# Where the softplus's sums and the fourth state's input run, in the last scan of a four-layer kernel

## The chip, the core and the metric

The kernel runs on one core of one Trainium2 chip, as one program without arithmetic on the host. The metric is the device time of one execution in microseconds; the median of three runs is given, and lower is better.

## The reference

Four residual layers work on four images of 128 channels and 128 x 128 pixels, in fp32. Each is x + layer(groupnorm(x)):

- layer 0: a deformable convolution (offsets from a 3 x 3 convolution, bilinear sampling at nine taps, a product with the weights);
- layer 1: a dilated 5 x 7 convolution to 16 channels and back to 128;
- layer 2: half of the channels go through a depthwise convolution, half through a selective scan in four directions over all 16384 pixels;
- layer 3: a 3 x 3 convolution less a difference of neighbours.

The change lies in layer 2's scan. Cut to it:

```python
dts = jnp.einsum('bkrl,kdr->bkdl', dts, dt_w)
delta = jax.nn.softplus(dts + dt_b[None, :, :, None])
def step(h, inp):
    u, d, b, c = inp
    dA = jnp.exp(d[..., None] * A)
    h = h * dA + (d * u)[..., None] * b[:, :, None, :]
    y = jnp.einsum('bkcn,bkn->bkc', h, c)
    return (h, y)
_, ys = lax.scan(step, h0, (u_l, d_l, B_l, C_l))
```

There are 128 channels, four directions k and 16 states n; the step runs over 16384 positions.

## The kernel before

**Blocks.** The scan of one image and direction is cut into 32 blocks of 512 positions, so there are 4 x 4 x 32 = 512 blocks in all, numbered through. A block has 128 channels x 16 states = 2048 rows. They are laid on the 128 partitions as four groups (g = 0 to 3) of 32 channels, each channel on four partitions; a group has four tiles along the free axis (ng = 0 to 3), called states here. One group is thus a tile h of 128 x 4 x 512.

**One group.** inputs_up (L893, ACT) copies delta*u of the group from the SBUF tile spread to the PSUM tile dub. DVE multiplies dub with the B values (L996), which makes the scan's inputs for the four states at once. ACT makes the decays exp(delta*A) into the PSUM tiles pa (L919), one a state, a little ahead. DVE scans each state (L1044). ACT saves the last column (carry, L953), POOL multiplies h by the C values, two states at a time (outputs, L959), and PE sums them over the partitions into yacc (sums, L933). One of the four inputs can be made apart: last_input (L899) has POOL multiply state 3 straight from spread, half a group ahead, and L996 then covers three states (1536 elements) in place of four (2048).

**The block after next.** While block t is scanned, the generator prepare(t + 2) makes its delta, one step at each state: PE makes pdt, ACT makes |x|, relu, exp(-|x|), 1 + e, ln(1 + e) (L841 to L854) and subtracts 1 again (L856). The softplus is relu + ln(1 + e) + (e - ((1 + e) - 1)), the last bracket a correction. These sums are made either by POOL in three instructions (L872, L874, L876), or on PE as four products with the identity or its negative into a PSUM tile psum (L867), copied back by ACT (L869). POOL then multiplies delta by u (L878); the result goes to DRAM and comes back spread out over the partitions. pdt, pxbc, psum and dub are all of one tag ("dub") of a pool with one buffer, so each waits for the reader of the one before.

**What runs beside.** The scan is the main loop. Between its states it pulls steps from the layers of the neighbouring images: beside the scan of image b run layer2_post and layer3 of image b - 1, and layer0, layer1 and layer2_pre of image b + 1. The wrapper loads() writes into beside["busy"] which engine the running stage loads: "POOL" for layer0 (whose gathers POOL issues), "PE" for layer1, layer2_pre and, in the earlier scans, layer2_post and layer3. In the last scan there is no next image; there layer2_post and layer3 of image 2 and layer2_post of image 3 run under the label None. So does the table that image 1's layer0 gathers from, early in the first scan.

**Order.** The instructions of each engine run in the order in which the program emits them (keep_order at the end holds it). Within a group of block t the loop over the states emits, for state 1: decays, outputs of the group before (second half), inputs_up for the next group if g > 1, sums of two groups before, a step of prepare; for state 2: carry_on, decays, last_input for the next group, a step of prepare, inputs_up if g < 2; for state 3: a step of prepare, outputs of this group (first half), sums of the group before. At states 1, 2 and 3 the scan itself is emitted after these. With on_pe the four PE products of prepare fall on state 1 of group 2 and the copy L869 on state 2 of that group, and inputs_up comes at state 2 in every group. Before the change on_pe holds beside layer0 alone, and last_input runs for odd g, wherever DVE doesn't take over part of the outputs (on_vector, again beside layer0 alone).

Of the kernel before, what the change touches and what calls it, by code (L numbers as in the profile page):

```python
# [111 lines left out]
def conv_preact_kernel(ctx: ExitStack, tc: tile.TileContext, a: dict, nb: int):  # L112
# [9 lines left out]
    def load(pool, src, shape, name, **kw):  # L122
        t = pool.tile(shape, F32, name=name, **kw)
        nc.sync.dma_start(t, src)
        return t
# [5 lines left out]
    beside = {}  # L131
# [64 lines left out]
    def blk(t, i):  # L196
        return t[:, i * N : (i + 1) * N]
# [593 lines left out]
    def scan(pull):  # L791
# [4 lines left out]
        seq = []  # L796
# [9 lines left out]
        def decays(at):  # L806

            beside["decays"] = lambda: decays(at + 1)
            while ahead["made"] < min(at + 2, len(seq) * NST):
                decay(ahead["made"])  # L810
                ahead["made"] += 1

        def fetch(t):
            if t < len(seq):
                st, k, i, _ = seq[t]
                while st.get("out", 0) < (i + 1 if k == 0 else NBLK + 1):
                    pull()
                    tick()
                if "y" not in st:
                    st["y"] = image("yrow"), image("ycol")  # L820
                us = st["u"]
                if not stored(us[0]):
                    flush()
                blocks[t]["u"] = load(sp, blk(us[k % 2], i), [P, N], "u", bufs=2)
# [57 lines left out]
        def spread_steps(t, g):  # L882

            blocks[t]["p", g] = p = sp.tile([P, 2, N], F32, name="spread", bufs=3)
            src = blocks[t]["steps"][g * Q : (g + 1) * Q]
            nc.sync.dma_start(
                p.rearrange("p j t -> p (j t)"), src.unsqueeze(1).to_broadcast([Q, P // Q, 2 * N])
            )

        def inputs_up(t, g):  # L890

            blocks[t]["pdu", g] = p = pss.tile([P, N], F32, name="dub", tag="dub")
            nc.scalar.copy(p, blocks[t]["p", g][:, 1, :])  # L893

        def last_input(t, g):

            c = blocks[t]
            c["h", g] = h = hp.tile([P, NG, N], F32, name="h")
            nc.gpsimd.tensor_mul(h[:, NG - 1, :], c["p", g][:, 1, :], c["bb"][:, NG - 1, :])  # L899

        def spread_states(t, what):

            blocks[t][what] = p = bp.tile([P, NG, N], F32, name=what)
            src = blocks[t]["bc"][("bb", "cb").index(what)].rearrange("(s n) t -> s (n t)", n=NG)
            nc.sync.dma_start(
                p.rearrange("p n t -> p (n t)"), src.unsqueeze(0).to_broadcast([Q, P // Q, NG * N])
            )
# [14 lines left out]
        def sums(t, g, half):  # L922

            c = blocks[t]
            second = seq[t][3]
            if g == 0 and half == 0:
                c["y"] = pss.tile([P, N], F32, name="yacc")
            last = g == NG - 1 and half == 1
            parts = (2 * half, 2 * half + 1)
            if half and c.get(("added", g)):  # L930
                parts = parts[:1]
            for ng in parts:
                nc.tensor.matmul(  # L933
                    c["y"], gather[:, g, :], c["h", g][:, ng, :],
                    start=g == 0 and ng == 0, stop=last and ng == parts[-1] and not second,
                )
            if last and second:
                nc.tensor.matmul(c["y"], ident, c["before"], start=False, stop=True)

        def finish(t):  # L940
            st, k, i, back = seq[t]
            y = sp.tile([P, N], F32, name="y", bufs=1)
            nc.scalar.copy(y, blocks[t]["y"])
            store(blk(st["y"][k % 2], i), y, of=st["y"])
            blocks[t] = None
            st["summed"] = t % (NDIR * NBLK) + 1 - 3 * NBLK

        def carry_on(t, g, half):

            end = 0 if seq[t][3] else N - 1  # L950
            n = g * NG + 2 * half
            h = blocks[t]["h", g][:, 2 * half : 2 * half + 2, :]
            nc.scalar.copy(blocks[t]["carry"][:, n : n + 2].unsqueeze(2), h[:, :, end : end + 1])  # L953

        def outputs(t, g, half, engine=nc.gpsimd):

            c = blocks[t]
            h = c["h", g][:, 2 * half : 2 * half + 2, :]
            engine.tensor_mul(h, h, c["cb"][:, 2 * half : 2 * half + 2, :])  # L959
            if half and g % 2 and beside.get("busy") == "PE":  # L960
                engine.tensor_add(h[:, 0, :], h[:, 0, :], h[:, 1, :])
                c["added", g] = True
# [17 lines left out]
        for t, (st, k, i, back) in enumerate(seq):  # L980
            c = blocks[t]
            carry = c["carry"]
            on_pe = beside.get("busy") == "POOL"
            more = prepare(t + 2, on_pe) if t + 2 < len(seq) else iter(())
            if t > 0:
                fetch(t + 3)
            for g in range(NG):
                then = (t, g + 1) if g + 1 < NG else (t + 1, 0)
                soon = (t, g + 2) if g + 2 < NG else (t + 1, g + 2 - NG)
                before = (t, g - 1) if g else (t - 1, NG - 1)  # L990
                earlier = (t, g - 2) if g > 1 else (t - 1, g + NG - 2)
                ready = ("h", g) in c
                if not ready:
                    c["h", g] = hp.tile([P, NG, N], F32, name="h")
                h, n = c["h", g], NG - 1 if ready else NG
                nc.vector.tensor_tensor(  # L996
                    h[:, 0:n, :], c["pdu", g].unsqueeze(1).to_broadcast([P, n, N]), c["bb"][:, 0:n, :], ALU.mult
                )
                on_vector = beside.get("busy") == "POOL"
                if before[0] >= 0:  # L1000
                    carry_on(*before, 1)
                if soon[0] < len(seq):
                    spread_steps(*soon)
                at = t * NST + g * NG
                decays(at)
                if g == 1:
                    if t + 1 < len(seq):
                        spread_states(t + 1, "bb")
                if g == 2 and t + 1 < len(seq):
                    spread_states(t + 1, "cb")  # L1010
                if g == 3 and back:
                    c["before"] = load(sp, blk(st["y"][k % 2], i), [P, N], "before", bufs=1)
                for ng in range(NG):
                    n = g * NG + ng
                    if ng == 1:
                        decays(at + 1)
                        if before[0] >= 0 and not on_vector:
                            outputs(*before, 1)
                        if g > 1 and then[0] < len(seq) and not on_pe:
                            inputs_up(*then)  # L1020
                        if earlier[0] >= 0:
                            sums(*earlier, 1)
                    if ng == 2 and g == 1 and t > 0:
                        finish(t - 1)
                    if n % NST and ng != 2:
                        next(more, None)
                    if ng == 2 and before[0] >= 0 and on_vector:
                        outputs(*before, 1, nc.vector)
                    if ng == 2:
                        carry_on(t, g, 0)  # L1030
                        decays(at + 2)
                        if g % 2 and not on_vector and then[0] < len(seq):
                            last_input(*then)
                        next(more, None)
                        if (g < 2 or on_pe) and then[0] < len(seq):
                            inputs_up(*then)
                    if ng == 3:
                        outputs(t, g, 0, nc.vector if on_vector and g == NG - 1 else nc.gpsimd)
                        if before[0] >= 0:
                            sums(*before, 0)  # L1040
                    o, f = h[:, ng, :], c["a", n]
                    if back:
                        o, f = o[:, ::-1], f[:, ::-1]
                    nc.vector.tensor_tensor_scan(o, f, o, carry[:, n : n + 1], ALU.mult, ALU.add)  # L1044
                    if ng == 3:
                        decays(at + 3)
                    yield (t * NST + n + 1) / slots
            for _ in more:
                pass
# [409 lines left out]
```

## Time and profile before

| what | value |
|---|---|
| median of three runs | 21988.68 us (21982.39 to 22019.09) |
| the profiled execution | 22048.69 us, its span 22046.9 us |
| busy over the span | PE 80%, DVE 81%, POOL 80%, ACT 74% |
| the scan on DVE, L1044 | 8192 instructions of 1267 ns |
| outputs on POOL, L959 | 3651 instructions of 2365 ns (445 more on DVE) |
| last_input on POOL, L899 | 845 instructions of 1278 ns |
| sums of the softplus on POOL, L872, L874, L876 | 423 of each, 1272 to 1283 ns |
| the same on PE, L867 | 89 blocks; each of the four products is two records of 592 ns |

An fp32 matmul stands in the trace as two records. The mean of PE's records includes the time in which one overlaps the next, so their sum is above PE's busy time. The last scan starts near 18000 us and ends near 21710 us; the convolution of image 3 follows until the end.

How to read the rows: a group's row gives line, engine and operation, what it writes and reads, the count; then busy time in us, the mean of one in ns, and how long the engine stood idle just before it and for whom. A row of the windows view gives, for a stretch of time, each engine's busy time and count of instructions, then the granted TensorE clock as a share of full speed, the busy share of the DMA engines, and GB/s.

### The profile page before, as it was taken

The page shows a single profiled execution, that of the slowest core. Times are in us where ns is not written, and L with a number is a line of the kernel's source. Part 1 is how long each engine was busy: PE and PEld are TensorE (multiplying, and loading weights), DVE is VectorE, ACT ScalarE, POOL GpSimd, SP SyncE. Part 2 cuts the span into 40 slices and gives each one's busy share as a digit, 9 for nine tenths or more (in the row PEclk, how much of TensorE's full clock was granted, in tenths as well). Part 3 has the DMA queues.
Part 4 walks back from the last instruction along what each step waited for, and adds up shares of the span by engine and source line. Part 5 has one row for each costly group of instructions (what it writes and reads, how often), then busy time and mean ns, then how long its engine had stood idle before and what let it go on. Part 6 is the DMA issues. An engine that isn't in the chain of part 4 may idle for free. (4 is left out here: it accounts for less than half of the span.)

```text
span 22046.9 us, 206313 instructions
## 1 busy us (share of the span) xinstructions
PE 17530.0 (80%) x51536; PEld 8506.2 (39%) x51536; DVE 17759.7 (81%) x18759; ACT 16420.1 (74%) x37439; POOL 17657.2 (80%) x11985
## 2 busy tenths in 40 slices
PE   4667777888878888788888887887887878778788
PEld 3444333445323333454533333344543333233333
DVE  2332688888998899888798889978889888999984
ACT  4775777888778776788868876688877877666673
POOL 3663787667899999777789999977779999999994
PEclk7888998999989999999999999999999999999999
DMA  7666678777766878777776697777776677556674
GB/s 226 189 187 185 191 241 274 245 242 246 255 207 221 237 242 266 243 246 243 246 249 216 219 262 240 257 245 240 250 252 219 221 224 228 200 202 209 214 233 134
DMA packets 2578940, 5040.76 MB, mean 229 GB/s; under 512 B 1060736, under 2 KB 1333576, under 8 KB 2435408
## 3 DMA queue, kind: packets, MB, share of 16 engines
q1 hardware_dynamic: 2209104, 3819.31, 53.2%
q0 software_dynamic: 368640, 1208.25, 18.1%
q8 instruction: 415, 6.80, 0.1%
q14 instruction: 781, 6.40, 0.1%
HBM read 4082.03 MB, written 874.52 MB: 225 GB/s over the span
## 5 line engine op out<-in xcount | busy, mean ns | idle before, releaser
L1044 DVE TENSOR_TENSOR_SCAN h<-pa,carry,h 128x512 f32<-128x512 f32 x8192 | 10011.3, 1267 | 605.7 <-ACT pa L919 386.4
L933 PE MATMUL yacc<-h,gather_sb 128*128 128x512 f32 x15264 | 7958.5, 648 | 1906.5 <-POOL h L959 1303.9
L959 POOL TENSOR_TENSOR h<-h,cb 128x1024 f32<-128x1024 f32 x3651 | 8589.1, 2365 | 622.3 <-ACT carry L953 575.2
L426 POOL DMA_INDIRECT g<-table,idx x4608 | 4535.8, 984 | 2470.2 <-issue 1174.3
L919 ACT ACTIVATE pa<-spread,neg_a 128x512 f32<-128x512 f32 x8192 | 5488.6, 682 | 109.9 <-DVE h L1044 82.3
L933 PEld LDWEIGHTS yacc<-h,gather_sb 128*128 128x128 f32 x15264 | 2967.8, 206 | 6073.5 <-issue 2925.7
L996 DVE TENSOR_TENSOR h<-dub,bb 128x2048 f32<-128x2048 f32 (+1 forms) x2048 | 4210.4, 2056 | 519.8 <-ACT dub L893 517.4
L464 PE MATMUL pst<-ident,g 128*128 128x128 f32 x9216 | 2134.8, 319 | 1327.6 <-ACT smp L469 1097.8
L440 ACT ACTIVATE g<-g,wt 128x128 f32<-128x128 f32 x9216 | 2839.4, 390 | 42.1 <-DMA g<-table,idx 38.9
L953 ACT COPY carry<-h 128x2 f32<-128x2 f32 x4096 | 769.5, 188 | 2705.7 <-DVE h L1044 2699.4
L464 PEld LDWEIGHTS pst<-ident,g 128*128 128x128 f32 x9216 | 1686.8, 224 | 2174.2 <-ACT smp L469 1614.3
L465 PE MATMUL pst<-ident,v 128*128 128x128 f32 x9216 | 2129.5, 318 | 321.9 <-DVE v L454 170.8
L451 DVE TENSOR_TENSOR pw<-pw,g 128x512 f32<-128x512 f32 x1152 | 797.0, 692 | 1961.2 <-ACT pw L440 1555.4
L465 PEld LDWEIGHTS pst<-ident,v 128*128 128x128 f32 x9216 | 1674.8, 227 | 419.2 <-DVE v L454 225.0
L440 ACT ACTIVATE pw<-g,wt 128x128 f32<-128x128 f32 x4608 | 1691.8, 367 | 131.7 <-DVE v L454 11.4
L893 ACT COPY dub<-spread 128x512 f32<-128x512 f32 x2048 | 1195.7, 584 | 302.4 <-DVE h L996 111.8
L454 DVE SCALAR_TENSOR_TENSOR v<-g,wt,pw 128x128 f32<-128x128 f32 x4608 | 1293.6, 343 | 114.4 <-issue 2.3
L475 PE MATMUL acc<-smp,w_sb 128*128 128x512 f32 x2304 | 1287.6, 642 | 21.4 <-DVE x L482 14.8
L469 ACT COPY smp<-pst 128x512 f32<-128x512 f32 x1152 | 668.1, 580 | 776.3 <-remote 578.2
L1264 PE MATMUL p<-xn,w_l_sb 128*128 128x508 f32 (+2 forms) x2304 | 1129.7, 608 | 1.8 <-ACT xn L1243 1.8
L899 POOL TENSOR_TENSOR h<-spread,bb 128x512 f32<-128x512 f32 x845 | 1079.5, 1278 | 15.9 <-DMA spread<-stepsd 10.2
L872 POOL TENSOR_TENSOR e<-e,one_e 128x512 f32<-128x512 f32 x423 | 538.2, 1272 | 486.8 <-ACT one_e L856 463.7
(183 smaller groups left out, 18935.7 us busy)
## 6 DMA issues: line engine op xcount, KB each, us to landing
spread<-stepsd SPq DMA_DIRECT2D x2048, 512.0 KB
bb<-bcd SPq DMA_DIRECT2D x512, 1024.0 KB
cb<-bcd SPq DMA_DIRECT2D x512, 1024.0 KB
stepsd<-steps SPq DMA_DIRECT2D x512, 512.0 KB
table<-gt SPq DMA_DIRECT2D x512, 256.0 KB
g<-table,idx POOLq DMA_INDIRECT x4608
u<-urow SPq DMA_DIRECT2D x256, 256.0 KB
yrow<-y SPq DMA_DIRECT2D x256, 256.0 KB
```

The source lines that it names most:

```text
L426: nc.gpsimd.indirect_dma_start(out=g[:, r].rearrange("p q c -> p (q c)"), out_offset=None, in_=table, in_offset=bass.IndirectOffsetOnAxis( ...
L440: nc.scalar.activation(pw[:, r * P : (r + 1) * P] if c == 0 else g[:, r, c, :], g[:, r, c, :], AF.Copy, scale=wv[:, r, q, k, c : c + 1],)
L454: nc.vector.scalar_tensor_tensor(v[:, r, :], g[:, r, 3, :], wv[:, r, q, k, 3:4], pw[:, r, :], ALU.mult, ALU.add)
L464: nc.tensor.matmul(dst, g[:, r, 2, :], ident, start=True, stop=False)
L465: nc.tensor.matmul(dst, v[:, r, :], ident, start=False, stop=True)
L475: nc.tensor.matmul(got["a", i], w0[:, k, :], got.pop(("c", n)), start=k == 0, stop=k == KK - 1)
L893: nc.scalar.copy(p, blocks[t]["p", g][:, 1, :])
L919: nc.scalar.activation(pa, blocks[t]["p", g][:, 0, :], AF.Exp, scale=neg_a[:, k, n : n + 1])
L933: nc.tensor.matmul(c["y"], gather[:, g, :], c["h", g][:, ng, :], start=g == 0 and ng == 0, stop=last and ng == parts[-1] and not second,)
L959: engine.tensor_mul(h, h, c["cb"][:, 2 * half : 2 * half + 2, :])
L996: nc.vector.tensor_tensor(h[:, 0:n, :], c["pdu", g].unsqueeze(1).to_broadcast([P, n, N]), c["bb"][:, 0:n, :], ALU.mult)
L1044: nc.vector.tensor_tensor_scan(o, f, o, carry[:, n : n + 1], ALU.mult, ALU.add)
```

## The change

Two conditions change. In a block, on_pe is now true unless the stage beside it is labelled "PE"; so it is true under "POOL", as before, and under None as well. And where on_pe is true and DVE doesn't take over outputs, last_input runs for the next group of every g in place of odd g alone. Under "POOL" and "PE" the program is as it was. Under None the sums of the softplus move from POOL to PE with ACT's copy, the inputs of state 3 of groups 1 and 3 move from DVE to POOL, and inputs_up moves from state 1 to state 2 in groups 2 and 3.

```diff
@@ -980,7 +980,7 @@
             carry = c["carry"]
-            on_pe = beside.get("busy") == "POOL"
+            on_pe = beside.get("busy") != "PE"
             more = prepare(t + 2, on_pe) if t + 2 < len(seq) else iter(())
@@ -1029,7 +1029,7 @@
                         carry_on(t, g, 0)
                         decays(at + 2)
-                        if g % 2 and not on_vector and then[0] < len(seq):
+                        if (g % 2 or on_pe) and not on_vector and then[0] < len(seq):
                             last_input(*then)
                         next(more, None)
                         if (g < 2 or on_pe) and then[0] < len(seq):
                             inputs_up(*then)
```

## The prediction

> **What bounds the kernel now.** I read the page's busy shares first (DVE 81%, POOL 80%, PE 80%: no single bound over the whole span), then the listing of both programs' instruction order, which says where the edit acts: the sum on PE goes from 89 of the 512 scan blocks to 228. The 139 new ones are blocks 25 to 38, beside image 1's table, and 388 to 512, the last scan. Then the windows view of those stretches; I cut the last scan where L1138 and L1264 come and go.
>
> ```profile
> core 0: us, PE busy (x) PEld busy (x) DVE busy (x) ACT busy (x) POOL busy (x), PEclk, DMA share, GB/s
> 18010.00:19110.00 1100.00, 865.94 (x1725) 332.03 (x1723) 986.11 (x744) 810.78 (x1599) 1079.66 (x626) 0.94 0.71 223
> 19110.00:20900.00 1790.00, 1417.47 (x3059) 576.08 (x3060) 1723.99 (x1301) 1138.97 (x2298) 1630.45 (x880) 0.95 0.61 206
> 20900.00:21710.00 810.00, 664.81 (x1342) 258.76 (x1341) 716.37 (x540) 591.47 (x1170) 786.89 (x456) 0.93 0.74 229
> 3040.00:3540.00 500.00, 328.58 (x753) 129.40 (x751) 438.38 (x365) 311.07 (x617) 386.64 (x210) 0.86 0.87 290
> ```
>
> I call them A (beside image 2's layer2_post), B (its layer3), C (image 3's layer2_post) and T (the table). L996 runs four times a block; its counts there are 142, 251, 103 and 60, so A has 35.5 blocks of 31.0 us, B 62.7 of 28.5, C 25.8 of 31.5, T 15 of 33.3. POOL is 98% and 97% busy in A and C, so POOL sets their pace; in B DVE is 96% busy and POOL 91%, so DVE does. After the scan only layer3 on PE is left, so a scan that ends earlier ends the kernel earlier.
>
> The groups of A (five rows; busy, mean ns, idle before), then of B (two):
>
> ```profile
> L959 POOL TENSOR_TENSOR h<-h,cb 128x1024 f32<-128x1024 f32 x177 | 415.8, 2364 | 9.3 <-ACT carry L953 9.3
> L996 DVE TENSOR_TENSOR h<-dub,bb 128x2048 f32<-128x2048 f32 x44 | 100.2, 2278 | 40.8 <-ACT dub L893 40.8
> L996 DVE TENSOR_TENSOR h<-dub,bb 128x1536 f32<-128x1536 f32 x44 | 76.7, 1743 | 8.0 <-ACT dub L893 8.0
> L899 POOL TENSOR_TENSOR h<-spread,bb 128x512 f32<-128x512 f32 x44 | 56.2, 1278 | 0.0
> L872 POOL TENSOR_TENSOR e<-e,one_e 128x512 f32<-128x512 f32 x22 | 28.2, 1281 | 5.9 <-ACT one_e L856 5.9
> ...
> L996 DVE TENSOR_TENSOR h<-dub,bb 128x2048 f32<-128x2048 f32 x99 | 225.5, 2277 | 16.0 <-ACT dub L893 16.0
> L996 DVE TENSOR_TENSOR h<-dub,bb 128x1536 f32<-128x1536 f32 x99 | 172.3, 1741 | 7.6 <-ACT dub L893 7.6
> ```
>
> The waits view (us, times, longest), A then B, shows PE's room:
>
> ```profile
> PE yacc L933 <- POOL h L959: 113.8, 60, 5.0
> ACT e L841 <- PE pdt L836: 36.6, 16, 7.0
> ...
> PE yacc L933 <- POOL h L959: 190.5, 123, 2.9
> DVE h L996 <- ACT dub L893: 23.6, 82, 0.7
> ```
>
> Over A's 22 blocks in that window PE waits for POOL 5.2 us a block, over B's 49.5 blocks 3.85. And one third group of B in the timeline (start, duration), where the new work will sit:
>
> ```profile
> 19915.51 1.88 PE L933 MATMUL yacc<-h,gather_sb 128*128 128x512 f32 x4
> 19916.18 1.76 DVE L996 TENSOR_TENSOR h<-dub,bb 128x1536 f32<-128x1536 f32 x1 [0.23 <-ACT dub L893]
> 19918.03 0.57 ACT L893 COPY dub<-spread 128x512 f32<-128x512 f32 x1
> 19918.04 4.81 DVE L1044 TENSOR_TENSOR_SCAN h<-pa,carry,h 128x512 f32<-128x512 f32 x4
> 19920.54 0.19 ACT L953 COPY carry<-h 128x2 f32<-128x2 f32 x1 [1.94 <-DVE h L1044]
> 19922.77 2.26 DVE L996 TENSOR_TENSOR h<-dub,bb 128x2048 f32<-128x2048 f32 x1
> ```
>
> ACT has the fourth group's dub ready 4 us before L996 takes it at 19922.77.
>
> [...] in the final layer3 PE makes 271 records in 100 us at "100% busy", yet one record lasts 0.59 us; back to back they start 0.43 us apart (timeline), and I count PE by that: 3059 records over B's 62.7 blocks are 49 a block, 21 of its 28.5 us. [...] I charge more PE work with no lower clock.
>
> **The change, per block.**
> *POOL.* Goes: L872, L874, L876, three of 1.28 us. Comes: last_input (L899) for groups 1 and 3 too, two of 1.28 us. L878 stays, one state later. Consecutive ones start 1.24 us apart (durations overlap), so POOL saves 1.24 us.
> *DVE.* Two L996 shrink from 2048 to 1536: 2 x (2278 - 1743) = 1.07 us less.
> *PE.* Four fp32 matmuls, two records each: 8 x 0.43 = 3.4 us, 3.6 with the tail. Covered by PE's waits for POOL: 5.2 us in A, 3.85 in B. B's cover is thin, 0.4 us.
> *ACT.* One PSUM copy, L869, taken at the 0.58 us of L893; ACT is 64 to 74% busy, so its room covers it. Its place in the order matters more than its length.
> *Order.* In groups 2 and 3 inputs_up moves from state 1 to state 2. psum shares its only buffer (tag dub) with the dub tiles: it cannot start before the third group's L996 has read dub, and the fourth group's dub cannot be written before L869 has read psum. From the L996 start of the third group: 1.74 + 3.6 (matmuls) + 0.58 (L869) + 0.59 (L893) + about 0.15 of handovers = 6.7 us. DVE wants the next dub after 1.74 + 4.81 = 6.55. So the fourth group starts 0.1 to 0.2 us late if PE is at the spot, later by whatever PE lags. Behind the waiting L869 stand dub, then pa for the fourth group's first states, which its scans need, and in A and C the side layer's copies. Group 3's own move is harmless: 1.74 + 2.43 + 0.19 + 0.68 + 0.59, under 5.8 us.
> *DMA, SP, buffers.* L878 one state later sends stepsd one tick later; its reader comes a block later. Spread tiles of groups 1 and 3 get POOL as a further reader, done before the group's last scan anyway. The h tile of groups 1 and 3 is taken half a group earlier, from a ring of five: its former user is five groups back. I cost these at nothing; the cover is that lead.
>
> **The sum.** B is DVE-paced: 1.07 less 0.25 (0.15 from the chain above, 0.1 for PE jitter) = 0.82; x 62.7 = 51 us. Busy there, POOL falls from 1630/62.7 = 26.0 to 24.8 us a block and DVE from 27.5 to 26.4, so DVE still binds. A and C are POOL-paced: 1.24 x 61.3 = 76 us if POOL never starves. It has stock: in A's timeline it ran the products of 18408.66 on states whose scans had ended near 18401.2, some 7 us before. DVE falls there to 27.8 - 1.07 = 26.7, under POOL's 29.2, but L869 and the side copies behind it can hold a fourth group some 2.5 us (the chain plus four 0.5 to 0.7 us activations), so the loop of DVE, ACT and PE comes near 29.5 itself; I take 0.8 of it, 61 us. T moves 345 GB/s at a full DMA share in its later two thirds; between 0 and 15 x 1.07 = 16 I take 8. Together 120 us: the profiled span goes from 22046.9 to about 21927, and the median, 60 us below the profiled execution's 22048.69, from 21988.7 to 21869; I say 21870. Ends: all of POOL's and DVE's saving kept, 76 + 67 + 16 = 159, or 189 if the dub stalls of B go as well (23.6 us in 49.5 blocks, 30 in 62.7); at the other end the chain eats B and half of A and C, and 20 to 40 are left.
>
> **Rivals.**
> *1. The chain takes it back.* psum, L869 and dub become the fourth group's pace; B gains nothing, A and C half: about -35 us, 21950. For: one buffer, zero slack, in-order ACT. Against: the timeline has PE idle or done at 19917.4, just before psum could start at 19917.9. Chance 0.16.
> *2. Slower: PE lags at psum.* Place: PE's queue ahead of the third group's psum, in B the convolution, in A three pd matmuls and sums that wait for POOL. Price: every us of lag is a us of DVE in each block of B. It decides from 1.07 - 0.15 + 76/62.7 = 2.1 us of mean lag in B with A and C kept, or less where they go too. At 3.5 us in B (the whole new PE work falling on DVE) and nothing kept elsewhere: 62.7 x (3.5 + 0.15 - 1.07) = +162, 22150; at 2.5 us, about +100. For: B's cover of 3.85 against 3.4, PE's union already 79%. Against: PE's 21 us by records become 24.5, of 27.7, and its waits for POOL are waits ahead of need, in which it can catch up. Chance 0.14.
> *3. The edit does little,* because the label is seldom empty: the order listing excludes it (139 blocks). Only T could be partly hidden.
>
> Forecast 0.70, whose own range is 21815 to 21930; rival 1 0.16; rival 2 0.14. The range of 21800 to 21985 takes in the ends and rival 1. What a measurement can tell from no change is 0.2%, 44 us: about half of rival 1 and a sliver of the forecast are within it. Faster 0.75, same 0.12, slower 0.13.
>
> **What would show it.** L872 falls to 284, L899 rises to 1129, L867 to 228 a form. Blocks: B near 27.7 us, A and C near 30. Right if POOL stays over 96% busy in A and C and L996's wait for dub in B stays under 0.7 us a block. Wrong if L869 waits over 2 us for PE in B, if POOL falls to 93% in A with L996 waiting for dub, or if PE passes 92% in B.

## The result and the profile after

The changed kernel takes 21888.24 us (median of 5 runs, 21877.65 to 21904.93), the kernel before beside it 21988.82 us: a ratio of 0.9952, with a 95% interval of 0.994 to 0.9963. That is 100.6 us less. The forecast was 21870 us, 119 us less.

The profiled span falls by 143.7 us, from 22046.9 to 21903.2. Only part of it is the change's. I took the start of each block (its first L996) from both traces; blocks are counted from 0, and block t makes the sums of block t + 2, so the prediction's blocks 25 to 38 are made in 22 to 35. From the start of block 386 to that of 511, the last scan, the kernel takes 92.3 us less (3725.9 to 3633.6 us); from the start of 22 to that of 36 (T) it takes 3.2 us less. The remaining 48 us lie in stretches where the two programs are the same, among them 17.6 us before block 22; the profiled execution of before had also been 60 us above its median. So some 95 us are to be explained.

The windows view of the kernel before and then of the kernel after, each cut at the starts of its blocks 386 and 422 (A), 422 and 484 (B), 486 and 511 (C), 22 and 36 (T). Columns: from and to, length, then busy time and records of each engine.

```profile
core 0: us, PE busy (x) PEld busy (x) DVE busy (x) ACT busy (x) POOL busy (x), PEclk, DMA share, GB/s
17958.00:19070.40 1112.40, 877.85 (x1746) 337.19 (x1746) 998.06 (x752) 818.39 (x1615) 1087.94 (x630) 0.94 0.71 224
19070.40:20840.70 1770.30, 1397.78 (x3019) 568.23 (x3018) 1705.91 (x1289) 1124.85 (x2269) 1615.92 (x872) 0.95 0.60 205
20898.00:21683.80 785.80, 643.99 (x1298) 250.63 (x1297) 692.48 (x522) 575.68 (x1138) 763.54 (x443) 0.93 0.75 233
3077.10:3532.00 454.90, 303.96 (x712) 120.42 (x712) 404.98 (x331) 287.49 (x574) 359.60 (x194) 0.87 0.90 302
...
17903.50:18991.90 1088.40, 964.17 (x2034) 389.60 (x2032) 963.52 (x753) 835.83 (x1651) 1043.63 (x594) 0.97 0.74 229
18991.90:20735.00 1743.10, 1550.23 (x3514) 650.32 (x3514) 1647.55 (x1288) 1153.72 (x2331) 1540.15 (x810) 0.98 0.61 208
20791.80:21537.10 745.30, 678.69 (x1484) 276.54 (x1482) 671.01 (x523) 585.70 (x1162) 732.53 (x418) 1.00 0.80 245
3059.50:3511.20 451.70, 337.43 (x824) 139.83 (x824) 391.04 (x331) 294.22 (x588) 342.43 (x180) 0.89 0.90 305
```

A, B and C hold 36, 62 and 25 blocks. A block goes from 30.90 to 30.23 us in A, from 28.55 to 28.11 in B and from 31.43 to 29.81 in C. (The lengths that the prediction divided by, 31.0, 28.5 and 31.5, came from windows cut by time.) POOL is now 95.9% busy in A, 88.4% in B and 98.3% in C; DVE is 94.5% busy in B. PE's clock rose, from 0.94, 0.95 and 0.93 to 0.97, 0.98 and 1.00.

The waits view (us, times, longest) of A, then B, then C:

```profile
DVE h L996 <- ACT dub L893: 69.5, 96, 4.8
ACT steps L869 <- PE psum L867: 60.0, 35, 5.7
PE yacc L933 <- POOL h L959: 42.8, 39, 3.3
POOL steps L878 <- ACT steps L869: 36.3, 17, 4.7
...
POOL steps L878 <- ACT steps L869: 140.4, 62, 5.4
DVE h L996 <- ACT dub L893: 61.4, 166, 3.7
ACT steps L869 <- PE psum L867: 47.2, 62, 4.0
PE yacc L933 <- POOL h L959: 18.8, 29, 1.2
...
DVE h L1044 <- ACT pa L919: 38.5, 24, 2.2
DVE h L996 <- ACT dub L893: 22.4, 71, 0.4
POOL steps L878 <- ACT steps L869: 10.3, 24, 1.5
```

PE used to wait for POOL in B, 261.4 us over the same blocks of the kernel before; what is left is 18.8 us. In its place stands a new chain of waits that follow each other: ACT at L869 for PE's products, POOL at L878 for ACT, DVE at L996 for the dub that stands behind L869. The third group of a block of B shows the links in the timeline (start, duration, what ended the idle time before):

```profile
19830.40 1.76 DVE L996 TENSOR_TENSOR h<-dub,bb 128x1536 f32<-128x1536 f32 x1 [0.23 <-ACT dub L893]
19832.27 4.81 DVE L1044 TENSOR_TENSOR_SCAN h<-pa,carry,h 128x512 f32<-128x512 f32 x4
19832.31 1.10 PE L867 MATMUL psum<-e,ident 128*128 128x512 f32 x2 [0.16 <-DVE h L996]
...
19834.96 1.02 PE L867 MATMUL psum<-steps,ident 128*128 128x512 f32 x2
19836.02 0.59 ACT L869 COPY steps<-psum 128x512 f32<-128x512 f32 x1 [0.47 <-PE psum L867]
19836.64 0.59 ACT L893 COPY dub<-spread 128x512 f32<-128x512 f32 x1
19836.68 1.28 POOL L878 TENSOR_TENSOR steps<-steps,u 128x512 f32<-128x512 f32 x1 [1.92 <-ACT steps L869]
19837.26 1.76 DVE L996 TENSOR_TENSOR h<-dub,bb 128x1536 f32<-128x1536 f32 x1 [0.18 <-ACT dub L893]
```

From the third group's L996 to the fourth's are 6.86 us; the scans end at 19837.08, so DVE stands 0.18 us. Here PE starts psum 0.15 us after L996, at once. POOL, which needs nothing of dub, stands 1.92 us.

The kernel before shows no wait ahead of a fourth group's L996; after, it is 0.46 us a block in B, 1.31 in A and 0.26 in C. The traces tell how it comes about. From PE's first product to the last one's end the chain takes 3.60 to 3.67 us in every block, and L869 and dub follow at once, with 0.04 and 0.03 us between them. What differs is when PE begins: on the average of the blocks it starts 0.47 us after the third group's L996 has ended in B, 1.52 in A, 0.30 in C, and at once, as above, means 0.15.

### The profile page after: what moved, and what is told of

Its sections match the earlier page's. It is cut to its first block, busy times and chain, and to the rows that moved or that the text cites. A ratio compares the mean times of both kernels' runs of the same rounds, so it can differ in the third digit from the quotient of the medians.

```text
span 21903.2 us, 208985 instructions
## 1 busy us (share of the span) xinstructions
PE 17833.1 (81%) x52648; PEld 8673.4 (40%) x52648; DVE 17623.7 (80%) x18759; ACT 16481.8 (75%) x37578; POOL 17478.3 (80%) x11852
## 5 line engine op out<-in xcount | busy, mean ns | idle before, releaser
L933 PE MATMUL yacc<-h,gather_sb 128*128 128x512 f32 x15264 | 7813.5, 639 | 1428.8 <-POOL h L959 719.6
L996 DVE TENSOR_TENSOR h<-dub,bb 128x1536 f32<-128x1536 f32 (+1 forms) x2048 | 4064.7, 1985 | 560.0 <-ACT dub L893 556.1
L899 POOL TENSOR_TENSOR h<-spread,bb 128x512 f32<-128x512 f32 x1129 | 1441.9, 1277 | 16.7 <-DMA spread<-stepsd 11.4
L878 POOL TENSOR_TENSOR steps<-steps,u 128x512 f32<-128x512 f32 x512 | 656.0, 1281 | 356.5 <-ACT steps L869 322.7
```

Source lines behind the costliest of these rows:

```text
L933: nc.tensor.matmul(c["y"], gather[:, g, :], c["h", g][:, ng, :], start=g == 0 and ng == 0, stop=last and ng == parts[-1] and not second,)
L996: nc.vector.tensor_tensor(h[:, 0:n, :], c["pdu", g].unsqueeze(1).to_broadcast([P, n, N]), c["bb"][:, 0:n, :], ALU.mult)
```

## The experiments

Each kernel ran beside the kernel before on the same chip; the diffs are against the changed kernel, where dots stand for lines left out. The medians of before differ between the sets of runs (21535 and 21536 us for all experiments but the last, 22064 for that, 21989 for the result), so ratios and stage times are compared. That stage times may be compared is itself measured, by running the changed kernel again:

> The changed kernel once more, on the chip of the next three: the base they are compared with. Ratio to before 0.994 to 0.997 under every theory; in the last scan (blocks 386 to 511) 3630 us within 8.

It took 21444.73 us against 21535.48: 0.9962 (0.9949 to 0.9976). Its last scan took 3627 us, against 3634 in the result, as was expected. This is one pair, and nearly all of its 6.4 us lies in B (4.9); A and C, which two of the experiments leave as they were, scatter over 3.6 and 0.3 us in four executions. So differences of less than about 7 us between single profiled executions are not read here. The stages of all kernels, in us of their profiled executions:

| kernel | A (36 blocks) | B (62) | C (25) | last scan (125) |
|---|---|---|---|---|
| before | 1112.4 | 1770.3 | 785.9 | 3725.9 |
| after | 1088.3 | 1743.2 | 745.3 | 3633.6 |
| after, again | 1087.0 | 1738.3 | 745.1 | 3627.2 |
| sums alone | 1093.9 | 1795.2 | 753.5 | 3700.6 |
| input alone | 1180.7 | 1785.1 | 833.6 | 3860.5 |
| du a step later | 1084.7 | 1737.8 | 745.0 | 3624.5 |
| own bank beside layer3 | 1084.7 | 1734.1 | 745.0 | 3620.5 |
| own bank, early products | 1085.1 | 1711.8 | 745.0 | 3598.7 |
| two products | 1062.4 | 1710.2 | 734.5 | 3563.2 |
| six products | 1139.0 | 1851.9 | 786.3 | 3837.4 |
| own bank in every stage | 1072.3 | 1712.2 | 739.6 | 3582.1 |

**Sums alone.** The sums go to PE; L996 keeps its four states in groups 1 and 3.

```diff
-                        if (g % 2 or on_pe) and not on_vector and then[0] < len(seq):
+                        if g % 2 and not on_vector and then[0] < len(seq):
```

> The softplus's sums go to PE under None; the fourth state's input stays on POOL for odd g alone. Theory M (stages: POOL paces A and C, DVE paces B): POOL has 3.7 us a block less, so A and C pass from POOL to the DVE, ACT and PE loop and run near 29.5 us a block (before 30.9 and 31.4, with the whole change 30.2 and 29.8), some 85 us gained there; B, which loses nothing on DVE and gets the late fourth group (0.3 to 0.5 us a block), gets 0 to 25 us slower. Sum against before: 50 to 90 us faster. Rival D (the shorter DVE inputs pay everywhere, the sums only cost): no faster than before, 0 to 40 us slower.

21524.65 us against 21536.46: 0.9995 (0.9987 to 1.0004), nothing that a measurement can tell. The windows of A, B and C say why:

```profile
17450.70:18544.70 1094.00, 962.25 (x2033) 388.98 (x2032) 999.76 (x753) 836.12 (x1651) 957.58 (x522) 0.97 0.73 227
18544.70:20339.90 1795.20, 1554.62 (x3514) 649.64 (x3514) 1711.17 (x1288) 1155.07 (x2331) 1392.27 (x686) 0.98 0.60 202
20397.80:21151.30 753.50, 679.30 (x1489) 277.17 (x1489) 695.08 (x522) 585.44 (x1162) 675.73 (x370) 1.00 0.79 243
```

Theory M's 50 to 90 us did not come. Rival D's "no faster" did, but not for its reason: A and C gained 18.5 and 32.4 us, so the sums don't only cost. They did not gain the 85 us of theory M, for there POOL is only 88% and 90% busy, and a block still takes 30.4 and 30.1 us in place of 29.5. There the pace has passed from POOL to the loop of DVE, ACT and PE: 27.8 us of DVE and 2.3 to 2.6 us in which it stands. In B, where DVE set the pace from the start, its busy time is about that of before (27.6 us a block against 27.5) and a block is 0.40 us longer: the price of the psum chain there with no DVE work taken away.

**Input alone.** Every group's fourth input goes to POOL; POOL keeps the sums as well.

```diff
-            on_pe = beside.get("busy") != "PE"
+            on_pe = beside.get("busy") == "POOL"
+            by_pool = beside.get("busy") != "PE"
...
-                        if (g % 2 or on_pe) and not on_vector and then[0] < len(seq):
+                        if (g % 2 or by_pool) and not on_vector and then[0] < len(seq):
```

> The fourth state's input of every group goes to POOL under None; the sums stay on POOL. Theory M: POOL gets 2.5 us a block more; A and C slow by about that (61 blocks, 130 to 150 us), in B POOL's 26.0 becomes 28.5 and takes over from DVE, B keeps its 28.5 or loses 0.5 us a block. Sum against before: 120 to 200 us slower. Rival D: DVE's 1.07 us a block over 125 blocks, 60 to 130 us faster than before.

21681.18 us: 1.0066 (1.0053 to 1.008), slower, and 145 us more than before, within the 120 to 200 expected. Its windows of A, B and C:

```profile
17462.00:18642.80 1180.80, 898.38 (x1743) 343.72 (x1741) 964.38 (x753) 818.95 (x1615) 1172.16 (x701) 0.92 0.68 211
18642.80:20427.80 1785.00, 1415.42 (x3018) 591.21 (x3018) 1642.46 (x1288) 1125.81 (x2269) 1761.83 (x997) 0.93 0.60 203
20488.90:21322.50 833.60, 673.34 (x1299) 262.13 (x1300) 668.24 (x523) 576.22 (x1138) 823.77 (x494) 0.90 0.71 220
```

POOL is 99% busy in all three, B included, and sets the pace everywhere; two instructions of 1.24 us more are 2.48 us a block, and A and C grew by 1.90 and 1.91. The two halves don't add: sums alone give -25.3 us in the last scan, the input alone +134.6, both together -92.3. The sums take off POOL what the input puts on it, and the input takes off DVE some of the time that the chain of the sums costs it.

**Du a step later.** L878 and what it sends come one step of prepare later under None.

```diff
                 nc.scalar.copy(delta, pd)
                 yield
+                if beside.get("busy") is None:
+                    yield
```

> After, with delta * u (L878) one step of prepare later under None, so that on POOL it stands behind the third group's first outputs and not ahead of them. Theory M: in A POOL stood idle 1.0 us a block before L878, in C 0.4, waiting for ACT's copy of psum; with other work ahead of it this wait goes: A 0.7 to 1.0 us a block faster, C 0.3, B unchanged since DVE paces it; 25 to 45 us faster than the changed kernel. Rival P (the wait shows only that PE is late, which then ends elsewhere): within 10 us of the changed kernel, with L996's wait for the fourth group's dub grown.

21437.02 us: 0.9955 (0.9941 to 0.9969), the ratio of the change itself; 2.7 us less in the last scan than the repeat of after, within its scatter. The rival held in the time, though not in its second half: L996's wait for dub in A did not grow (67.2 us, against 69.5). The groups of A show where POOL's idle time went (busy, mean ns, idle before; lines are shifted by 2, so these are outputs and the product with u):

```profile
L961 POOL TENSOR_TENSOR h<-h,cb 128x1024 f32<-128x1024 f32 x289 | 681.5, 2368 | 30.0 <-ACT carry L955 29.3
L880 POOL TENSOR_TENSOR steps<-steps,u 128x512 f32<-128x512 f32 x36 | 46.1, 1282 | 11.0 <-ACT steps L869 11.0
```

The wait moved from L878 (36.3 us) to the outputs, which now wait for the carry, copied after the scan; POOL stands 1.14 us a block, against 1.24. In A there is no stock that a later L878 could draw on: POOL waits for the loop, wherever in its queue L878 stands.

**Own bank beside layer3.** Beside layer3 a PSUM bank that other stages use (bank 2) is free, and psum takes it in place of the shared buffer. The matmuls need no longer wait for L996, nor dub for L869's read, but the order of emission stays.

```diff
-                pd = pss.tile([P, N], F32, name="psum", tag="dub")
+                pd = bank(2, "psum") if beside.get("free") else pss.tile([P, N], F32, name="psum", tag="dub")
...
-            return [(post, 16), (loads(load, conv, True), 22)]
+            return [(post, 16), (loads(load, conv, True, True), 22)]
```

> After, with psum in a PSUM bank of its own (bank 2, which layer3 leaves free) beside layer3 in the last scan, so in B alone; elsewhere it shares the dub buffer as in the changed kernel. Theory M (the one buffer makes the fourth group late): L996's idle before the fourth group falls from 0.46 us a block to 0.1 or less, B gets 0.2 to 0.4 us a block shorter, 10 to 25 us faster than the changed kernel. Rival P (PE's lag, not the buffer, makes it late, since ACT's copy of psum stands ahead of dub in ACT's order anyway): the idle stays at 0.3 or more and B within 0.1 us a block.

21428.87 us: 0.9949 (0.9935 to 0.9962). B fell by 9.1 us against after, 4.2 against its repeat: at most 0.15 us a block. DVE's wait ahead of the fourth group is 0.36 us, against 0.46 in the result but 0.37 in the repeat, so the buffer alone brings nothing that can be told, as the rival had it. L869 still stands ahead of dub in ACT's queue: with the buffers apart, as with the shared one in the result, dub is ACT's next instruction after L869 in all 62 blocks of B. It starts 0.48 to 0.62 us after L869 does, in the result 0.61 to 0.62. That is the "in-order ACT" of rival 1, as far as it was measured.

**Own bank, early products.** As above, and beside layer3 the four products are emitted two steps earlier, while L869 stays where it was.

```diff
-                yield
-                yield
-                pd = bank(2, "psum") if beside.get("free") else pss.tile([P, N], F32, name="psum", tag="dub")
+                free = beside.get("free")
+                if not free:
+                    yield
+                    yield
+                pd = bank(2, "psum") if free else pss.tile([P, N], F32, name="psum", tag="dub")
...
+                if free:
+                    yield
+                    yield
                 yield
                 nc.scalar.copy(delta, pd)
```

> Beside layer3 in the last scan (B) psum has its own PSUM bank, and PE's four products are emitted two states earlier, in group 1, with ACT's copy where it was: PE's work is the same, the chain from the third group's L996 over the products to the fourth group's dub is gone. Theory M (that chain makes the fourth group late): L996's idle before the fourth group in B falls from 0.46 us a block to 0.1 or less, ACT's copy no longer waits for PE, B 0.3 to 0.4 us a block shorter, 15 to 25 us faster than the changed kernel. Rival W (PE's added work, not its place, delays DVE): the idle moves to the second and third groups, B within 0.1 us a block.

21412.83 us: 0.9945 (0.9931 to 0.9959). All five of its times lie under all five of the repeat, which ran beside it. B takes 27.61 us a block, 0.43 less than in the repeat of after and 0.51 less than in the result, somewhat more than the 15 to 25 us expected, and the fourth group's wait for dub is down to 0.06 us. The waits view of its B (lines shifted by 5 from L869 on; L869 is here the products, L874 the copy, L1001 the inputs):

```profile
POOL steps L883 <- ACT steps L874: 95.4, 62, 3.7
PE psum L869 <- ACT one_e L856: 86.5, 54, 2.4
DVE h L1001 <- ACT dub L898: 36.9, 111, 2.0
```

ACT's 62 waits for the products have become 6, of 6.5 us together. PE now waits 1.4 us a block for one_e, ahead of need, and DVE's waits for dub fell from 61.4 to 36.9 us. All four products are kept, only their buffer and place differ, and about half a microsecond a block comes back: what B lost, it lost to the chain, and not to the work that PE was given.

**Two products and six products.** The chain's length alone. The first leaves out the two products of the correction e - ((1 + e) - 1) under None; the second adds e and takes it off again.

```diff
+                use = [(e, ident), (one_e, less), (ln, ident), (delta, ident)]
+                if beside.get("busy") is None:
+                    use = use[2:]
```

```diff
+                use = [(e, ident), (one_e, less), (ln, ident), (delta, ident)]
+                if beside.get("busy") is None:
+                    use += [(e, ident), (e, less)]
```

> Under None the sum on PE has two products in place of four; the correction term of the softplus (e less what is left of 1 + e) is left out there. The chain before the fourth group's dub is 1.7 us shorter. Theory M: L996's idle before the fourth group goes to 0.1 us a block or less in B and to 0.5 or less in A; B 0.3 to 0.45 us a block shorter (about 22 us), A 0.3 to 0.8 (10 to 30 us), C little; 30 to 55 us faster than the changed kernel. Rival P (POOL alone paces A and C): A and C unchanged, 15 to 25 us from B alone.

> Under None the sum on PE has six products, the last two adding e and taking it away again: the chain is 1.7 us longer. Theory M (no slack in the chain): the fourth group starts 1.5 to 1.8 us later in every block of B, 95 to 110 us over B; in A and C 0.7 to 1.5 us a block, 45 to 90 us; 140 to 200 us slower than the changed kernel, so slower than before. Rival H (a microsecond or two of slack hides it): 0 to 50 us slower than the changed kernel.

Two products: 21377.82 us, 0.9927 (0.9913 to 0.994). Six: 21670.72 us, 1.0064 (1.005 to 1.0078), slower than the kernel before. Two products are four records 0.43 us apart, 1.7 us of chain. Taking them away gives 0.72 us a block in A, 0.53 in B, 0.43 in C against the result; adding them costs 1.41, 1.75 and 1.64 us. Both moved the time by more than was expected: against the repeat, by medians, 67 us less (30 to 55) and 226 us more (140 to 200). So with four products the chain is at the edge: over four fifths of a longer chain is paid, and a shorter one only brings what was being paid for it. The waits view of the six, B then C (lines shifted by 3):

```profile
POOL steps L881 <- ACT steps L872: 249.5, 62, 6.0
DVE h L999 <- ACT dub L896: 170.2, 168, 4.1
ACT steps L872 <- PE psum L870: 156.4, 62, 4.3
...
DVE h L999 <- ACT dub L896: 63.5, 71, 2.0
ACT steps L872 <- PE psum L870: 54.6, 24, 2.3
POOL steps L881 <- ACT steps L872: 51.5, 24, 3.2
```

In C, POOL had been 98.3% busy, and still the longer chain cost 41.0 us over 25 blocks, while POOL's wait at the product with u rose from 10.3 to 51.5 us. A full engine gave no cover: the loop through psum was about as long, and when it grew, it set the pace (31.5 us a block, with POOL busy for 29.3).

**Own bank in every stage.** The early products everywhere: beside layer3 as before, and beside layer2_post with the bank of the decays' third buffer, so that decays keep two.

```diff
+                pd = bank(free, "psum") if free else pss.tile([P, N], F32, name="psum", tag="dub")
...
-        post, conv = loads(load, layer2_post(sts[b], engine), True), layer3(sts[b])
+        post = loads(load, layer2_post(sts[b], engine), bool(load), 0 if load else 3)
...
-        return side + [(loads(None, layer2_post(sts[b]), True), rounds)]
+        return side + [(loads(None, layer2_post(sts[b]), False, 3), rounds)]
```

> As e5_early_products in B; beside the two layer2_post (A and C) psum takes the bank that held the third decay tile, so there the decays have two buffers in place of three, and the products stand two states earlier too. Theory M: L996's idle before the fourth group (1.26 us a block in A, 0.26 in C) goes to 0.1, and POOL's wait before L878 with it; if two decay buffers are enough, A gets 0.5 to 0.7 us a block and C 0.3 to 0.45 shorter (as with two products), 25 to 35 us faster than e5_early_products. Rival B (the third decay buffer carries A and C): the scans' waits for pa, 1.5 and 2.1 us a block, grow by more than what is saved; 0 to 60 us slower than e5_early_products.

21929.79 us against 22063.58: 0.994 (0.9926 to 0.9953). Rival B did not hold: the missing decay buffer costs DVE some waits (1.41 us a block in A at the scans, for pa, against 1.01 in the result) but less than the chain did, and DVE's wait ahead of the fourth group is gone in all three stages. A block takes 29.79 us in A and 29.58 in C; the last scan is 17 us shorter than with the early products in B alone, less than the 25 to 35 expected. The whole last scan takes 3582 us, the shortest of the kernels that keep all the sums, 45 us under the repeat of after. The interval of its ratio reaches into that of the change's, so the full times alone don't prove it the faster of the two; the stage times, of one profiled execution each, speak for it by more than their scatter.

## Why the prediction was right, and where its sum was off

The direction and the mechanism held: POOL set the pace of A and C, DVE of B, each lost work, and a chain over psum, L869 and dub took part of it back. The end moved by as much as the last scan did. The terms:

| stage | predicted gain | measured gain |
|---|---|---|
| A and C | 61 us, 0.99 a block | 64.7 us: A 0.67, C 1.62 a block |
| B | 51 us, 0.82 a block | 27.1 us, 0.44 a block |
| T | 8 us | 3.2 us |
| together | 120 us | 95.0 us |

The two blocks between B and C gave 0.5 us more. That A and C together came so near the forecast is luck: A gave a third less than the 0.99, C two thirds more, and the sum foresaw neither.

**B, the term that was mis-sized.** "1.07 less 0.25 (0.15 from the chain above, 0.1 for PE jitter)". DVE's busy time fell by 0.94 us a block (27.51 to 26.57), not 1.07: L996's own records fell by 64.2 us in 62 blocks, 1.04 a block, nearly as foretold; but successive instructions of DVE overlap in the records (added up they are 1.2 us a block more than their union before, 1.1 after), and the busy time, the union, fell by less. And the stall was 0.50 us, not 0.25 (DVE's idle time 1.04 to 1.54 a block). Sums alone, +0.40, and the early products, -0.43 to -0.51, put the same size on it from two sides. The chain's 6.7 us against 6.55 was nearly right (6.86 in the block above), and where PE is at the spot the fourth group waits 0.18 us, with 0.15 foretold. What was too low was the allowance for a PE that isn't: on the average of B it began 0.47 us after L996, so 0.32 later than at the spot, where the prediction allowed 0.1 of jitter, and the wait is 0.46 in place of 0.18. (Its argument that PE was "idle or done at 19917.4" overlooks a convolution product of the layer beside, from 19917.22 to 19918.23; in the new order that product stands behind the sums, so it is not what made PE late.) ACT's waits for PE at L869 are 47.2 us in 62 blocks, the longest 4.0. So the test "L996's wait for dub in B stays under 0.7 us a block" failed, with 61.4/62 = 0.99; before it was 30.6/62 = 0.49 over the same blocks. In the steady middle of B, blocks 440 to 480, PE began 0.27 us after L996 and the stall grew by only 0.31; in the first 18 blocks of B it began 0.85 us after. What makes PE late there is not shown.

**A.** "It has stock", and of the moved L878, "I cost these at nothing; the cover is that lead". L878 stands in POOL's own queue: POOL waits there 36.3 us, 1.01 a block, and its idle time in all grew from 0.68 to 1.24. Of the 1.23 us that POOL was spared 0.67 are left. Du a step later shows that the lead itself is missing in A, not only its order. The discount of 0.8 should have been near a half there, and it was the chain that took the rest: with two products less A gets back 0.72 us. The 29.5 us that the prediction had for the loop of DVE, ACT and PE is not refuted: sums alone takes 30.4 with a DVE that works 1.01 us more a block, so 29.4 is an estimate from these two for the loop after. With POOL's busy 29.0 beside it, a block took 30.2; how the two add up to that is not shown. Some blocks went the way of rival 2, PE lagging at psum; on the average of A it began 1.52 us after L996. In the timeline of one of them:

```profile
18234.49 3.45 PE L933 MATMUL yacc<-h,gather_sb 128*128 128x512 f32 x4 [2.84 <-ACT carry L953]
18237.74 1.27 PE L1113 MATMUL pd<-yrl,cmat_sb 128*128 128x512 f32 x2
...
18243.13 1.02 PE L867 MATMUL psum<-e,ident 128*128 128x512 f32 x2
18247.43 1.28 POOL L878 TENSOR_TENSOR steps<-steps,u 128x512 f32<-128x512 f32 x1 [4.68 <-ACT steps L869]
```

PE stood 2.84 us for the sums; they then took 3.45 us, at a granted clock of 0.55 of full speed (18234.49 to 18237.74), against 1.88 us at 1.00 for four such records in the block of B above (from 19830.26); and the pd products of the layer beside stood ahead of psum. POOL paid 4.68 us.

**C, where the sum left out a gain.** Before, the first of the three sums on POOL, L872, waited there for ACT. From the waits view of the kernel before, in C:

```profile
POOL e L872 <- ACT one_e L856: 20.4, 24, 2.8
```

That is 0.82 us a block. It went with the instruction, and the new wait at L878 costs only 0.41: 1.24 + 0.89 - 0.51 (POOL's idle time before and after) = 1.62, the measured gain. The prediction priced the instructions removed from POOL but not the wait at their head. Why L878's wait is less than half as long a block in C as in A is not shown beyond PE's being nearer the spot there (0.30 us against 1.52).

**T.** The gain of 8 us was a guess between 0 and 16; the 3.2 us found are within the scatter of single executions. In T a wait of about 23 us at the switch to layer0 stands in both kernels, before at DVE's work for layer0, after at dub, since layer0's first products on PE, which wait 18.7 us for a DMA, stand ahead of psum. It moved and did not go.

**The rivals.** Rival 1 had the right place, the chain, and for A the right size: A kept about half. But B kept nearly half where it foretold nothing, and C gained more than all. Rival 2 needed a mean lag of 2.1 us in B; it was 0.32.

**The other tests.** L872 fell to 284, L899 rose to 1129 and L867 is 456 records a form, 228 blocks of two. Blocks of 30.2 and 29.8 us in A and C and 28.1 in B were near the 30 and 27.7 foretold. "POOL stays over 96% busy in A and C" came to 95.9% and 98.3%, so it just failed in A. L869 waits 0.76 us a block in B, under the 2, and PE is 88.9% busy there, under the 92. That PE's work would bring no lower clock, an assumption of the author's, held on the average: PEclk rose in every stage, from 0.94 to 0.97 in A, 0.95 to 0.98 in B, 0.93 to 1.00 in C and 0.87 to 0.89 in T. Single stretches lie far lower: in the block of A above it was 0.55 for 3.25 us, after PE had stood 2.84 us. Why is not shown.

## What to carry to other kernels

Price a moved sum by the chain that its buffer and its place in the queues make, and not by the busy time of the engine that takes it: the four products were 3.6 us of a PE with room, and yet two more of them turned a gain of 0.5% into a loss of 0.6%. A full engine need not be the only one that sets the pace: in C POOL was 98.3% busy, and 1.7 us more of chain still cost 1.64 us a block. When an instruction is taken away, count the wait at its head too. Two edits of which each pays for what the other costs have to be judged together: 0.9995 and 1.0066 alone, 0.9952 both.

## What was not expected of the hardware

The TensorE clock rose where PE got more work: with eight records more a block PEclk in C went from 0.93 to 1.00, where PE went from 82% to 91% busy. The busy share alone doesn't fix it: in the kernel before, PE was 79% busy in B at a PEclk of 0.95, and 82% busy in C at 0.93.

The same program took 21535, 21989 or 22064 us in different sets of runs. For the changed kernel, profiled in the first two of these (21441.3 and 21903.2 us), 288 of the 462 us arise in layer 0 of the first image (0 to 2000 us: PEclk 0.88 against 0.80, 222 against 199 GB/s), and 30, 68 and 72 in the three stretches of the scan beside which layer 0 of the next image runs; the last scan is the same within 0.2%. Why layer 0 alone differs so is open.
